# A state-space scan with a planner that writes the order: the carried column is copied later, GpSimd's product gets its own buffer, and the planner chooses its next step differently

## The chip, the cores and the metric

The kernel runs on one core of a Trainium2 chip. Five engines have a queue of instructions each and work through it in order: TensorE (PE in the profile; PEld are its weight loads), VectorE (DVE), ScalarE (ACT), GpSimd (POOL) and SyncE (SP), which here only issues DMAs. They wait for each other through semaphores. The metric is the time of one execution on the device, in microseconds, as the median of several runs.

## The reference

A layer with two parts, on `u` of 4 sequences x 2048 steps x 256, all in f32:

```python
x = u + ssm(layernorm(u))
out = x + moe(layernorm(x))

# ssm, per sequence; 512 inner channels, 16 states per channel
xi, z = split(v @ W_in.T + b_in)
dt_raw, B, C = split(xi @ W_x.T + b_x)            # 16, 16, 16 wide
delta = softplus(dt_raw @ W_dt.T + b_dt)
h[t] = exp(delta[t] * A) * h[t-1] + xi[t] * delta[t] * B[t]
y[t] = sum_n h[t] * C[t]
ssm = ((y + xi * D) * silu(z)) @ W_out.T + b_out

# moe: 4 experts that share Wi and Wo and differ by a rank-4 addition
w = top-2 of softmax(x @ Wg.T + bg)
moe = sum_e w_e * (relu(x @ Wi.T + low_e @ Bm_e) @ Wo.T)
```

## The kernel before, in words

**Tiles.** The 8192 steps are cut into 16 chunks of `TC = 512` steps, four chunks to a sequence. Inner channels lie on the partitions, in four blocks `d` of 128, and time lies along the free dimension. A *state* is one pair of channel block and state number, 128 channels x 512 steps; a chunk has 4 x 16 = 64 of them, the kernel 1024. The list `states` (line 775) sets their sequence: half a chunk has two channel blocks, and within it a group of four states is two state numbers of the one block and then of the other.

**One state.** ScalarE makes the decay `dA = exp(delta * A)` into one of three PSUM buffers (`decay`, 783). GpSimd makes `dBx = xdt * B` for two states at once (`enter`, 788). VectorE runs the recurrence with one scan instruction, written over `dA` (`scan`, 800). The scan begins from the last column of the same state in the chunk before, kept in the small tile `carry`; ScalarE copies that column there (`keep`, 822). The last chunk of a sequence (3, 7, 11, 15) copies nothing, and the first (0, 4, 8, 12) begins from zero. Then the result is multiplied by C (`read`, 814) and TensorE adds it, transposed, into the PSUM tile `y` (`sum_y`, 827). For one state in four (`shared`, 809: the first of each group) the scan writes to `hS` in SBUF, and GpSimd does the product with C, in place; for the other three VectorE does it, from PSUM into `hC` (three buffers).

**The rest of a chunk.** In front of the scans of a chunk stand its layer norm (statistics `st_a` on VectorE, `rstd` on GpSimd, `xn_a` on ScalarE), the input projection (`pin`), the projection `pdbc`, whose B and C rows go through DRAM and are loaded back spread over the partitions, and softplus over the whole chunk. The gate is made with silu. Behind the scans come the gating of `y` (`close_y`), the output projection `po` (`tail`), and the mixture of experts (`ffn`): a layer norm, the routing in small tiles (`plg`, `m`, `lowm`), and eight steps `k` of base and low-rank products (`pz`), relu (`h`), transposes (`phT`, `hT`) and a down product (`pf`). While the scans of chunk c run, the front of chunk c+1 and the mixture of experts of chunk c-1 are worked on by whatever engine has time. Exp and relu, softplus, and silu need different tables, so softplus and silu each stand between two `ACT_TABLE_LOAD`s.

**The order.** Nothing is reordered after recording: each engine executes in the order in which Python writes the instructions. The main loop (915 to 976) writes the scan's own instructions state by state. Everything else is a list of `Step`s (35), each with an engine, an assumed cost in us, the steps that it follows, and the PSUM banks it takes and gives. `Pacer` (45) keeps an assumed clock for each engine. `start` (74) says when a step could begin by these clocks; `ready` (127) says whether it falls in a window around VectorE's clock. `fill` (106), called twice per state, writes all steps that are ready: the first ready one of the first thread, again and again. `force` (139) writes what a certain step needs, for instance where the next chunk is due, and at the end of the program, first for the second-last store and then for the last.

**The place of the copy.** In the loop's turn `i` the copy for state `i - 1` is written first (921), then the scan of state `i`, then fillers, then the C product of state `i - 1`, then the decay of state `i + 2`, then fillers. The tile framework lets two engines read one PSUM bank only one behind the other, in the order of recording, so the C product of VectorE waits for the copy.

Of the kernel before, what the change touches and what calls it, by code (L numbers as in the profile page):

```python
# [8 lines left out]
F32 = mybir.dt.float32  # L9
AF = mybir.ActivationFunctionType  # L10
ALU = mybir.AluOpType
# [33 lines left out]
class Pacer:  # L45
# [60 lines left out]
    def fill(self):  # L106

        begin = self.now["dve"]
        again = True
        while again:  # L110
            again = False
            for thread in self.threads:
                for x in self.heads(thread):
                    if (x.engine != "dve" or self.fits(x, begin)) and self.ready(x):
                        self.write(x)
                        thread.remove(x)
                        again = True
                        break
                if again:
                    break  # L120
        self.threads = [t for t in self.threads if t]

    def fits(self, x, begin):
# [3 lines left out]
    def ready(self, x):  # L127
        t = self.start(x)
        if t is None:
            return False  # L130
        v = self.now["dve"]
        if self.quiet and x.engine == "act" and x.cost > self.MOST:
            return False
        if x.engine == "dve":
            t = max([y.end for y in x.after if y.engine != "dve"], default=0.0)
            return t + self.LATENCY + self.MARGIN <= v
        return t <= v + self.BEGIN[x.engine] and (t + x.cost <= v + self.END[x.engine] or t <= v - 0.5)

    def force(self, last):

# [20 lines left out]
def ssm_moe_layer_kernel(  # L161
# [154 lines left out]
    def layernorm_T(src, dst, name, then=None):  # L316

        q = {}

        def stats(j):  # L320
            if j == 0:
                q["mv"] = small.tile([P, NJ, 2], F32, tag=f"mv{name[0]}", name=f"mv_{name}")
            x = small.tile([P, 6], F32, tag="st", name=f"st_{name}_{j}")
            dve.bn_stats(x, src()[:, j, :])
            dve.bn_aggr(q["mv"][:, j, :], x)

        def rstd():

            ve = small.tile([P, NJ], F32, tag="ve", name=f"ve_{name}")
            q["rstd"] = small.tile([P, NJ], F32, tag="rstd", name=f"rstd_{name}")  # L330
            q["nmr"] = small.tile([P, NJ], F32, tag="nmr", name=f"nmr_{name}")
            pool.tensor_scalar_add(ve, q["mv"][:, :, 1], EPS)
            pool.tensor_tensor(q["rstd"], ve, mhalf, ALU.pow)
            pool.tensor_tensor(ve, q["mv"][:, :, 0], q["rstd"], ALU.mult)
            pool.tensor_scalar_mul(q["nmr"], ve, -1.0)

        def norm(j):
            q["xn", j] = work.tile([P, DM], F32, tag=f"xn{j}", name=f"xn_{name}_{j}", bufs=1)
            act.activation(
                q["xn", j], src()[:, j, :], AF.Identity,  # L340
                scale=q["rstd"][:, j : j + 1], bias=q["nmr"][:, j : j + 1],
            )

        def turn(k):
            q["pt", k] = mm_tile(f"pt_{name}_{k}")
            for j in range(NJ):
                pe.transpose(
                    q["pt", k][:, j * P : (j + 1) * P], q["xn", j][:, k * P : (k + 1) * P], ident
                )

        def out_(k):
            if k == 0:
                q["dst"] = dst()
            act.copy(q["dst"][:, k, :], q["pt", k])

        steps = [Step("dve", 0.54, lambda j=j: stats(j)) for j in range(NJ)]
        steps += [Step("pool", 1.75, rstd)]
        steps += [Step("act", 0.5, lambda j=j: norm(j), locks=j == 0) for j in range(NJ)]
        norms = steps[-1]
        turns = [  # L360
            Step("pe", 0.45, lambda k=k: turn(k), after=[norms], takes=1, unlocks=k == KM - 1)
            for k in range(KM)
        ]
        outs = [Step("act", 0.5, lambda k=k: out_(k), after=[turns[k]], gives=1) for k in range(KM)]
        if then:
            steps.append(then)
        return steps + turns + outs
# [16 lines left out]
    def front(c, norm, taken=()):  # L384
# [65 lines left out]
        ln = steps[-1]  # L450
        for x in steps[-2 * KM :]:
            x.after += taken
        steps.append(Step("pe", 1.75, p_dbc, after=[ln], takes=1))
        steps.append(Step("act", 0.57, a_dbc, gives=1))
        dbc = steps[-1]
        dts, ins = [], []
# [5 lines left out]
        for m in range(ND):  # L462
# [2 lines left out]

        steps += dts + [soft] + ins if c == 0 else ins + dts + [soft]
        xdts = [
            Step("pool", 1.27, lambda m=m: xdt(m), after=[soft, ins[2 * m + 1]]) for m in range(ND)
        ]
        steps += xdts  # L470
        gate = []
# [78 lines left out]
    def ffn(c):  # L550
# [163 lines left out]
        for x in steps[-2 * KM :]:  # L714
            x.after += held.get("x2T", [])
        steps += [
            Step("pe", 2.0, p_route, takes=1),
            Step("act", 0.21, low_),
            Step("dve", 0.34, logits),
            Step("act", 0.85, exp_),  # L720
            Step("dve", 1.9, softmax, gives=1),
            Step("pool", 1.0, top),
            Step("pool", 0.6, mask),
            Step("pe", 0.5, p_turn, takes=1),
            Step("act", 0.5, a_turn, gives=1),
# [7 lines left out]
        for k in range(NK + 1):  # L733

            low = Step(
                "pe", 1.06 if 0 < k < NK else 0.9, lambda k=k: p_low(k), after=bases[k : k + 1] + z1s[-1:]
            )
            steps.append(low)
            if k:
                hs.append(Step("act", 0.57, lambda k=k: a_relu(k - 1, 0), after=[low], gives=1))  # L740
                steps.append(hs[-1])
            if k < NK:
                z1s.append(Step("act", 0.57, lambda k=k: a_relu(k, 1), after=[low]))
                steps.append(z1s[-1])
            steps += bases[k + 1 : k + 2]
            if k:
                steps.append(Step("pe", 0.9, lambda k=k: p_hT(k - 1), after=[hs[-1]], takes=1))
                steps.append(Step("act", 0.5, lambda k=k: a_hT(k - 1), after=[steps[-1]], gives=1))
                copies.append(steps[-1])
            for j in range(NJ):  # L750
                if k == min(2 * j + 3, NK):
                    for h in range(2):
                        steps.append(
                            Step("pe", 1.75, lambda j=j, h=h: p_down(j, h), after=[copies[2 * j + 1]], takes=1 - h)
                        )
                    steps.append(Step("dve", 0.33, lambda j=j: add(j), after=[steps[-1]], gives=1))
# [43 lines left out]
    def scan(i):  # L800
        c, ib, d, n = states[i]
        init = 0.0 if c % CPB == 0 else carry[:, d, n : n + 1]
        out_ = dAs[i]
        if shared(i):
            out_ = hCs[i] = scanp.tile([P, TC], F32, tag="hS", name=f"hS_{i}", bufs=2)
        dve.tensor_tensor_scan(out_, dAs[i], dBxs.pop(i), init, ALU.mult, ALU.add)
        dAs[i] = out_

# [5 lines left out]
    def read(i):  # L814
        c, ib, d, n = states[i]
        if shared(i):
            pool.tensor_tensor(hCs[i], hCs[i], bcs[ib, 1][:, n % NN, :], ALU.mult)
            return
        hCs[i] = scanp.tile([P, TC], F32, tag="hC", name=f"hC_{i}", bufs=3)
        dve.tensor_tensor(hCs[i], dAs.pop(i), bcs[ib, 1][:, n % NN, :], ALU.mult)  # L820

    def keep(i):
        c, _, d, n = states[i]
        if (c + 1) % CPB:
            act.copy(carry[:, d, n : n + 1], dAs[i][:, TC - 1 : TC])

    def sum_y(i):

# [80 lines left out]
    for d in range(ND2):  # L909
        scale, turn = open_y(0, d)  # L910
        xd = pacer.run("act", 0.63, scale)
        pacer.run("pe", 0.5, turn, [xd])
    begin(0)
    xds, turn, summed = {}, None, []
    for i in range(M + 4):

        pacer.quiet = (i + 5) % (PER // NH) < 8
        if turn:
            pacer.run("pe", 0.5, *turn)
            turn = None  # L920
        if 1 <= i <= M:
            pacer.run("act", 0.15, lambda: keep(i - 1), [S[i - 1]])
        for e in (1, 4):

            if i + e < M + 3 and i + e >= 3:
# [5 lines left out]
        if 3 <= i < M + 3:  # L931
            c, _, d, n = states[i - 3]
            if n == N - 1:
                copy, *steps = close_y(c, d)
                steps[0].after = [pacer.run("act", 0.5, copy, [Y[i - 3]]), silus[c]]
                pacer.add(steps, first=True)
                gates.setdefault(c, []).append(steps[-1])
                turn = xds.pop((c + 1, d - ND2) if d >= ND2 else (c, d + ND2), None)
                if d == ND - 1:
                    begin(c + 1)  # L940
# [19 lines left out]
        if 1 <= i <= M:  # L960
            if shared(i - 1):
                C[i - 1] = pacer.run("pool", 1.23, lambda: read(i - 1), [S[i - 1]])
            else:
                C[i - 1] = pacer.run("dve", 0.6, lambda: read(i - 1), [S[i - 1], *summed[-3:-2]])
            if i + AHEAD_A < M:
                A[i + AHEAD_A] = pacer.run(
                    "act", 0.63, lambda: decay(i + AHEAD_A), [(S if shared(i - 1) else C)[i - 1]]
                )
        for late in (3, 2):
            if late <= i < M + late and (late == 3) == shared(i - late):  # L970
                Y[i - late] = pacer.run("pe", 0.5, lambda: sum_y(i - late), [C[i - late]])
                if late == 2:
                    summed.append(Y[i - late])
        if i < M:
            group(i)
        pacer.fill()
    pacer.force(before_last)
    pacer.force(last_out)


# [45 lines left out]
```

## Time and profile before

| | us |
|---|---|
| median of 3 runs | 2138.67 (2132.21 to 2139.30) |
| the profiled execution | 2132.56 |
| its span | 2130.8 |
| first to last scan | 31.8 to 2000.8 |
| behind the last scan | 130.0 |

| engine | busy us | share | instructions |
|---|---|---|---|
| TensorE | 1875.5 | 88% | 9504 |
| VectorE | 1848.2 | 87% | 2423 |
| GpSimd | 1708.3 | 80% | 1084 |
| ScalarE | 1427.2 | 67% | 2898 |

| costliest groups | count | mean us | busy us |
|---|---|---|---|
| GpSimd dBx | 512 | 2.365 | 1206.3 |
| VectorE scan into dA, from carry | 576 | 1.277 | 723.5 |
| ScalarE dA | 1024 | 0.690 | 704.3 |
| VectorE hC | 768 | 0.675 | 518.1 |
| GpSimd hS | 256 | 1.274 | 326.2 |
| ScalarE carry from dA | 576 | 0.156 | 89.7 |
| ScalarE table load | 64 | 1.283 | 82.1 |

How to read it: busy time is the time in which an engine executes. On VectorE and ScalarE an instruction that waits for nothing begins a little before the one ahead ends, so distances of starts are shorter than durations: 1.19 us for a scan of 1.28, 0.60 for a product of 0.67. A line of the waits says which engine stood idle before which instruction, and what released it at last. In the text chunks are counted from 0, states within a chunk from 0 to 63.

### The profile page before, as it was taken

What the parts mean: (1) busy time and instruction counts of PE and PEld (TensorE: products, weight loads), DVE (VectorE), ACT (ScalarE), POOL (GpSimd) and SP (SyncE); (2) the same over time, 40 slices, a digit from 0 to 9 for tenths busy, and PEclk for the clock granted to TensorE, in tenths of its full rate; (3) what the DMA queues carried; (4) which work ended last, traced back from release to release, by engine and by line L of the source; (5) the groups of instructions that cost most, each with busy time, mean ns of one, the idle gap of its engine ahead of it and who ended that gap; (6) DMA issues with size and microseconds to landing.
All of it is one profiled execution on the core that took longest, in us unless ns stands there. A gap on an engine that the chain in (4) does not pass through costs nothing. (4 is left out here: it accounts for less than half of the span.)

```text
span 2130.8 us, 28679 instructions
## 1 busy us (share of the span) xinstructions
PE 1875.5 (88%) x9504; PEld 1284.4 (60%) x9504; DVE 1848.2 (87%) x2423; ACT 1427.2 (67%) x2898; POOL 1708.3 (80%) x1084
## 2 busy tenths in 40 slices
PE   6768788798898898999999898988999899989878
PEld 3545556566566575656666565666657566666655
DVE  4899899999999999999999998989999899899510
ACT  5757667667767777766777776666777767766422
POOL 5898888889888887998898887879888888988400
PEclk9859799899899999999999998999999999999989
DMA  6444344444444453543544353444535444443100
GB/s 213 152 161 151 128 149 143 157 147 158 141 148 151 138 179 118 179 140 140 169 148 160 132 175 115 143 150 145 174 129 179 139 137 143 147 159 139 50 11 10
DMA packets 106133, 300.71 MB, mean 141 GB/s; under 512 B 12864, under 2 KB 39104, under 8 KB 105984
## 3 DMA queue, kind: packets, MB, share of 16 engines
q1 hardware_dynamic: 105984, 298.88, 41.3%
q8 instruction: 74, 1.21, 0.2%
q14 instruction: 75, 0.61, 0.1%
HBM read 289.41 MB, written 9.44 MB: 140 GB/s over the span
## 5 line engine op out<-in xcount | busy, mean ns | idle before, releaser
L30 POOL TENSOR_TENSOR dBx<-xdt,B 128x1024 f32<-128x1024 f32 x512 | 1206.3, 2365 | 92.3 <-DVE dA L30 38.0
L30 ACT ACTIVATE dA<-delta,a_sb 128x512 f32<-128x512 f32 x1024 | 704.3, 690 | 364.7 <-DVE hC L30 336.7
L30 DVE TENSOR_TENSOR_SCAN dA<-dA,carry,dBx 128x512 f32<-128x512 f32 x576 | 723.5, 1277 | 26.3 <-ACT carry L30 14.6
L30 DVE TENSOR_TENSOR hC<-dA,C 128x512 f32<-128x512 f32 x768 | 518.1, 675 | 84.8 <-ACT carry L30 81.8
L30 PE MATMUL y<-ident,hC 128*128 128x128 f32 x3072 | 486.6, 289 | 33.8 <-DVE hC L30 33.1
L30 PEld LDWEIGHTS y<-ident,hC 128*128 128x128 f32 x3072 | 384.2, 149 | 179.8 <-DVE hC L30 65.9
L30 POOL TENSOR_TENSOR hS<-hS,C 128x512 f32<-128x512 f32 x256 | 326.2, 1274 | 76.5 <-ACT carry L30 60.1
L30 PE MATMUL pz<-wi_sb,x2T 128*128 128x512 f32 x512 | 267.4, 648 | 17.4 <-ACT hT L30 11.3
L30 PE MATMUL pf<-wo_sb,hT 128*128 128x256 f32 x1024 | 244.7, 386 | 11.4 <-ACT hT L30 8.5
L30 PE MATMUL pin<-xnT,w_in_sb 128*128 128x512 f32 x512 | 246.0, 609 | 2.7 <-ACT lowT L30 1.1
L30 DVE TENSOR_TENSOR_SCAN hS<-dA,carry,dBx 128x512 f32<-128x512 f32 x192 | 243.9, 1270 | 3.2 <-ACT dA L30 3.1
L30 DVE TENSOR_TENSOR_SCAN dA<-dA,dBx 128x512 f32<-128x512 f32 x192 | 228.8, 1216 | 2.0 <-ACT carry L30 1.9
L30 ACT ACTIVATE h<-pz,topv 128x512 f32<-128x512 f32 x256 | 168.2, 686 | 89.2 <-PE pz L30 87.4
L30 PEld LDWEIGHTS pf<-wo_sb,hT 128*128 128x128 f32 x1024 | 188.5, 192 | 38.6 <-ACT hT L30 12.4
L30 PE MATMUL y<-ident,hS 128*128 128x128 f32 x1024 | 169.8, 292 | 39.5 <-POOL hS L30 39.5
L30 PEld LDWEIGHTS y<-ident,hS 128*128 128x128 f32 x1024 | 129.5, 149 | 119.7 <-POOL hS L30 54.8
L30 PEld LDWEIGHTS pz<-wi_sb,x2T 128*128 128x128 f32 x512 | 94.1, 205 | 129.1 <-issue 80.1
L30 PE MATMUL phT<-ident,h 128*128 128x128 f32 x1024 | 142.6, 283 | 29.5 <-ACT h L30 19.0
L30 PE MATMUL pz<-bm_sb,lowT 16*128 16x512 f32 x512 | 165.9, 653 | 0.0
L30 PEld LDWEIGHTS phT<-ident,h 128*128 128x128 f32 x1024 | 119.8, 145 | 57.3 <-ACT h L30 23.8
L30 PEld LDWEIGHTS pin<-xnT,w_in_sb 128*128 128x128 f32 x512 | 92.5, 198 | 83.2 <-issue 71.8
L30 PE MATMUL po<-w_out_sb,g 128*128 128x256 f32 x512 | 128.6, 401 | 5.7 <-DVE u L30 2.7
(94 smaller groups left out, 1750.9 us busy)
## 6 DMA issues: line engine op xcount, KB each, us to landing
B<-bc SPq DMA_DIRECT2D x256, 512.0 KB, 3.7
C<-bc SPq DMA_DIRECT2D x256, 512.0 KB, 3.8
ua<-in_u_dram SPq DMA_DIRECT2D x16, 512.0 KB, 5.6
u<-in_u_dram SPq DMA_DIRECT2D x16, 512.0 KB, 5.5
out_dram<-u SPq DMA_DIRECT2D x16, 512.0 KB, 3.4
w_in_sb<-in_w_inT_dram SPq DMA_DIRECT2D x2, 512.0 KB, 4.7
wi_sb<-in_wiT_dram SPq DMA_DIRECT2D x1, 1024.0 KB, 8.0
wo_sb<-in_woT_dram SPq DMA_DIRECT2D x1, 1024.0 KB, 11.2
```

The source lines that it names most:

```text
L30: return self._tc.keep_in_program_order(f(*args, **kwargs))
```

## The change

The copy of the column is written behind the product with C (behind GpSimd's product for the states that GpSimd multiplies), directly ahead of the next decay. GpSimd's product goes into a tile of its own, `hP`, with two buffers, in place of being written over `hS`. `hC` has four buffers, not three, and the product waits in the planner for the fourth-last sum, not the third-last. `fill` makes a list of all ready steps and writes the one whose engine would stand idle the least before it (0.25 us of idleness count as none; among equals the first thread wins). At the end `drain` takes over from the two calls of `force`: of all steps that can be written, the one that begins earliest. Silu of a chunk is forced before the chunk's first `y` is closed. Some assumed costs are changed. The program has the same compute instructions; the order is made anew throughout.

```diff
     def fill(self):
         begin = self.now["dve"]
-        again = True
-        while again:
-            again = False
-            for thread in self.threads:
-                for x in self.heads(thread):
-                    if (x.engine != "dve" or self.fits(x, begin)) and self.ready(x):
-                        self.write(x)
-                        thread.remove(x)
-                        again = True
-                        break
-                if again:
-                    break
+        while True:
+            due = [
+                (max(0.0, self.start(x) - self.now[x.engine] - 0.25), at, x)
+                for at, thread in enumerate(self.threads) for x in self.heads(thread)
+                if (x.engine != "dve" or self.fits(x, begin)) and self.ready(x)
+            ]
+            if not due:
+                break
+            _, at, x = min(due, key=lambda d: d[:2])
+            self.write(x)
+            self.threads[at].remove(x)
...
+    def drain(self):
+        while self.threads:
+            heads = [(x, t) for t in reversed(self.threads) for x in self.heads(t) if self.start(x) is not None]
+            x, thread = min(heads, key=lambda h: self.start(h[0]))
+            self.write(x)
+            thread.remove(x)
+            self.threads = [t for t in self.threads if t]
...
-        steps += [Step("pool", 1.75, rstd)]
+        steps += [Step("pool", 1.95, rstd)]
...
-            out_ = hCs[i] = scanp.tile([P, TC], F32, tag="hS", name=f"hS_{i}", bufs=2)
+            out_ = scanp.tile([P, TC], F32, tag="hS", name=f"hS_{i}", bufs=2)
...
     def read(i):
         c, ib, d, n = states[i]
         if shared(i):
-            pool.tensor_tensor(hCs[i], hCs[i], bcs[ib, 1][:, n % NN, :], ALU.mult)
+            hCs[i] = scanp.tile([P, TC], F32, tag="hP", name=f"hP_{i}", bufs=2)
+            pool.tensor_tensor(hCs[i], dAs[i], bcs[ib, 1][:, n % NN, :], ALU.mult)
             return
-        hCs[i] = scanp.tile([P, TC], F32, tag="hC", name=f"hC_{i}", bufs=3)
-        dve.tensor_tensor(hCs[i], dAs.pop(i), bcs[ib, 1][:, n % NN, :], ALU.mult)
+        hCs[i] = scanp.tile([P, TC], F32, tag="hC", name=f"hC_{i}", bufs=4)
+        dve.tensor_tensor(hCs[i], dAs[i], bcs[ib, 1][:, n % NN, :], ALU.mult)
...
-            act.copy(carry[:, d, n : n + 1], dAs[i][:, TC - 1 : TC])
+            act.copy(carry[:, d, n : n + 1], dAs.pop(i)[:, TC - 1 : TC])
...
-        if 1 <= i <= M:
-            pacer.run("act", 0.15, lambda: keep(i - 1), [S[i - 1]])
...
+                pacer.force(silus[c])
...
-                C[i - 1] = pacer.run("dve", 0.6, lambda: read(i - 1), [S[i - 1], *summed[-3:-2]])
+                C[i - 1] = pacer.run("dve", 0.6, lambda: read(i - 1), [S[i - 1], *summed[-4:-3]])
+            pacer.run("act", 0.1, lambda: keep(i - 1), [(S if shared(i - 1) else C)[i - 1]])
             if i + AHEAD_A < M:
                 A[i + AHEAD_A] = pacer.run(
...
-    pacer.force(before_last)
-    pacer.force(last_out)
+    pacer.drain()
```

The other assumed costs: `p_dbc` 1.75 to 1.86, `xdt` 1.27 to 1.23, `p_route` 2.0 to 1.75, `top` 1.0 to 1.1, the first and last `p_low` 0.9 to 1.05, `p_hT` 0.9 to 0.88, and 0.5 to 0.45 for `sum_y` and the opening transposes.

More of the change, by code (lines that the diff above doesn't have):

```diff
@@ L452, in front @@
             x.after += taken
-        steps.append(Step("pe", 1.75, p_dbc, after=[ln], takes=1))
+        steps.append(Step("pe", 1.86, p_dbc, after=[ln], takes=1))
         steps.append(Step("act", 0.57, a_dbc, gives=1))
@@ L467, in front @@
         xdts = [
-            Step("pool", 1.27, lambda m=m: xdt(m), after=[soft, ins[2 * m + 1]]) for m in range(ND)
+            Step("pool", 1.23, lambda m=m: xdt(m), after=[soft, ins[2 * m + 1]]) for m in range(ND)
         ]
@@ L716, in ffn @@
         steps += [
-            Step("pe", 2.0, p_route, takes=1),
+            Step("pe", 1.75, p_route, takes=1),
             Step("act", 0.21, low_),
@@ L721, in ffn @@
             Step("dve", 1.9, softmax, gives=1),
-            Step("pool", 1.0, top),
+            Step("pool", 1.1, top),
             Step("pool", 0.6, mask),
@@ L735, in ffn @@
             low = Step(
-                "pe", 1.06 if 0 < k < NK else 0.9, lambda k=k: p_low(k), after=bases[k : k + 1] + z1s[-1:]
+                "pe", 1.06 if 0 < k < NK else 1.05, lambda k=k: p_low(k), after=bases[k : k + 1] + z1s[-1:]
             )
@@ L746, in ffn @@
             if k:
-                steps.append(Step("pe", 0.9, lambda k=k: p_hT(k - 1), after=[hs[-1]], takes=1))
+                steps.append(Step("pe", 0.88, lambda k=k: p_hT(k - 1), after=[hs[-1]], takes=1))
                 steps.append(Step("act", 0.5, lambda k=k: a_hT(k - 1), after=[steps[-1]], gives=1))
@@ L911, in ssm_moe_layer_kernel @@
         xd = pacer.run("act", 0.63, scale)
-        pacer.run("pe", 0.5, turn, [xd])
+        pacer.run("pe", 0.45, turn, [xd])
     begin(0)
@@ L918, in ssm_moe_layer_kernel @@
         if turn:
-            pacer.run("pe", 0.5, *turn)
+            pacer.run("pe", 0.45, *turn)
             turn = None
-        if 1 <= i <= M:
-            pacer.run("act", 0.15, lambda: keep(i - 1), [S[i - 1]])
         for e in (1, 4):
@@ L970, in ssm_moe_layer_kernel @@
             if late <= i < M + late and (late == 3) == shared(i - late):
-                Y[i - late] = pacer.run("pe", 0.5, lambda: sum_y(i - late), [C[i - late]])
+                Y[i - late] = pacer.run("pe", 0.45, lambda: sum_y(i - late), [C[i - late]])
                 if late == 2:
```

## The prediction

> **What bounds the kernel now.** I read the busy table first, then the windows of one chunk each, then the waits of VectorE, then the timeline around the longest waits, then the chain that ends last.
>
> ```profile
> PE 1875.5 (88%) x9504; PEld 1284.4 (60%) x9504; DVE 1848.2 (87%) x2423; ACT 1427.2 (67%) x2898; POOL 1708.3 (80%) x1084
> ```
>
> No engine is full, so the bound must be read by stage. The scans run from 31.8 to 2000.8 us (1969.0 us, VectorE busy 1832.0); behind them stands a tail of 130.0 us with VectorE busy 11.8. The scan stage is VectorE's: idle 137.0 us. Windows of VectorE alone (stretch, length, busy, then clock and DMA) show where:
>
> ```profile
> 274.60:399.90 125.30, 116.26 (x152) 0.90 0.42 148
> 399.90:515.60 115.70, 113.55 (x140) 0.99 0.44 151
> 1385.70:1510.50 124.80, 116.17 (x153) 0.96 0.43 148
> ```
>
> These are chunks 2, 3 and 11. Chunks 3, 7, 11 and 15 end a sequence and copy no carried column. Their idle time is 2.2, 5.6, 8.6 and 5.4 us, 21.7 in all (mean 5.4). The twelve that copy have 115.3, mean 9.6. The waits of VectorE and one of GpSimd name the difference (total, times, longest):
>
> ```profile
> DVE hC L30 <- ACT carry L30: 81.8, 79, 6.1
> DVE dA L30 <- ACT carry L30: 16.4, 15, 2.9
> DVE dA L30 <- ACT dA L30: 10.0, 17, 1.4
> POOL hS L30 <- ACT carry L30: 60.1, 73, 4.3
> ```
>
> The C product waits for ScalarE's copy of one column, since both read the same PSUM tile and the copy is recorded first. ScalarE works in order, so whatever stands ahead of the copy holds VectorE. Silu in chunk 9, a carrying one (start, length):
>
> ```profile
> 1148.73 1.28 ACT L30 ACT_TABLE_LOAD   x1
> ...
> 1150.03 1.92 ACT L30 ACTIVATE g<-g 128x2048 f32<-128x2048 f32 x1
> ...
> 1151.95 1.28 ACT L30 ACT_TABLE_LOAD   x1
> 1153.24 0.69 ACT L30 ACTIVATE dA<-delta,a_sb 128x512 f32<-128x512 f32 x1
> 1153.87 0.15 ACT L30 COPY carry<-dA 128x1 f32<-128x1 f32 x1
> 1154.06 0.69 DVE L30 TENSOR_TENSOR hC<-dA,C 128x512 f32<-128x512 f32 x1 [2.29 <-ACT carry L30]
> ```
>
> ScalarE is held 4.5 us (1148.73 to 1153.24), and the product then waits for a decay and the copy behind it: 2.29 us lost. The same block at the same state of chunk 11, without copies, ends so:
>
> ```profile
> 1407.50 1.30 ACT L30 ACTIVATE dA<-delta,a_sb 128x512 f32<-128x512 f32 x2
> 1408.30 1.28 DVE L30 TENSOR_TENSOR_SCAN hS<-dA,carry,dBx 128x512 f32<-128x512 f32 x1 [1.18 <-ACT dA L30]
> ```
>
> Products went on; only the scan waited for its decay: 1.18 us. So the copy costs 1.1 us at such a block, and there are two blocks per chunk.
>
> **The change, part by part.** *The copy behind the product.* In the built program 576 C products wait for ScalarE before, none after. If carrying chunks idle like the others, 12 x (9.6 - 5.4) = 50 us go. Ends: 0 (the waits only change their name) and 98.2 (81.8 + 16.4, all of it). I take 50, the row of the chunks without copies being the nearest there is.
>
> What it adds: the copy now waits for the product, and the decay stands behind it. In a group of four states VectorE runs: scan 0, product of the last group's state 3, scan 1, scan 2, product 1, scan 3, product 2. The decay for scan 2 needed scan 0 alone; now the copy of the last group's state 3 is ahead of it on ScalarE. From that product's start: 0.67 product, 0.15 copy, 0.69 decay, three handovers of about 0.04 (scan 712 ended 1401.51, its decay began 1401.55): 1.63 us. Scan 2 is due 0.60 + 1.19 = 1.79 us after that start. The slack of this one decay falls from about 0.95 to 0.16; the others keep about 0.7, where the copy had some 0.2 twice a group. One decay per group, 16 groups, 12 chunks: 192 tight places. Ends: 0 if ScalarE is free each time, 192 x (0.69 - 0.16) = 102 us if an activation of 0.69 has always just begun. ScalarE is busy 1375.9 of 1969.0 us in this stage (70%), but most fillers are placed where the old order had slack; chunks without copies, with 0.16 to 0.95 us more slack, waited for decays 1.8 to 4.5 us per chunk. I take 0.05 us per place: +10.
>
> Also, 292 decays now wait for the copy directly ahead on their own engine: the next activation starts 0.15 + 0.03 instead of 0.04 us behind the copy (1144.44 to 1144.48), so 292 x 0.14 = 41 us more of ScalarE over twelve chunks, 3.4 each of 116, within its 30% idle: 0 on the path beyond the 10. Here the Trainium skill (ScalarE: Activation LUTs, What ACT_TABLE_LOAD costs) speaks against the change: back-to-back activations overlap by about 93 ns, which a wait for the instruction ahead gives up; by it the estimate is 292 x 0.09 = 27 us of ScalarE. The same section prices a table load at about 2.7 us; by it a block would last 7.3 us and the two blocks of every chunk would take 32 x 2.8 = 90 us more than the trace has. The trace has 1.28, and it decides.
>
> *GpSimd's own buffer hP.* Its wait of 60.1 us for the copy goes. GpSimd reaches VectorE through dBx and hS alone, and VectorE's waits for those are 3.8 + 1.4 + 0.2 = 5.4 us: gain 0 to 5.4. I take 0, as the 3.8 is the start of the first scan. *Fourth hC buffer:* the product's waits for TensorE are 1.0 us in all: 0 to 1.0, taken 0. *Silu forced before the y of its chunk closes:* in the new order silu stands at state 5 of its chunk from chunk 6 on, and the force falls at state 32, so it finds nothing to do: 0. *Step costs* move only the order.
>
> *The new fill rule.* The order is made anew on all engines, the loads of SP and GpSimd's small steps included. From chunk 7 on softplus stands at state 24 of every chunk and silu at state 5, where before they wandered from 12 to 17 and 28 to 39. At state 24 all four statistics pairs of the next chunk (4 x 0.5 us: 0.32 to 0.41 and 0.18) stand inside the block, so most of its loss is covered; silu at 5 has two gate products (0.67) and I expect 1.9 us lost. SP's loads of B and C stand some nine states ahead of their readers in both orders, and VectorE waited 1.4 us for them: 0. GpSimd's bias add stands further behind its load (its waits for that DMA were 25.9 us), which does not reach VectorE. The remaining idle time, 16 x 5.4 = 86, bounds the gain: at best chunk 3's 2.2 everywhere (-52); at worst chunk 10's 13.7 (its window 129.9, busy 116.2) everywhere (+133). Most of a chunk is as before, so I take -10.
>
> *The tail.* At the last scan the new program has two of FFN 14's eight steps less to do, and the first four matmuls of the output product come ahead of the last down product. A step costs (2106.98 - 2094.90) / 2 = 6.0 us:
>
> ```profile
> 2094.90 3.72 PE pf L30 x16
> ...
> 2106.98 3.72 PE pf L30 x16
> ```
>
> So -12, between 0 (TensorE ends the scans behind) and -12 - 6.3 (the output product `po`, 6.33 us, wholly beside other work). TensorE has room for it in the scans: 1744.7 busy of 1969.0.
>
> Sum: -50 + 10 + 0 - 10 - 12 = -62 against the profiled execution's 2132.6 us (span 2130.8, 1.8 around it): 2070.6. That execution lies at the low end of the runs (2132.21 to 2139.30, median 2138.67), so I say 2072 for a median.
>
> **The rivals.** *The decays become the wait (slower).* Place: the decay for scan 2 of each group. If ScalarE is late there by 0.37 us on average over the 192 places, 71 us come back and, with the forecast's 72 of gains, nothing is left; at 0.5 us, 96 come back: 2132.6 - 72 + 96 = 2157. For it: slack 0.16 against fillers of 0.6 to 0.7 us, 256 of them `h`, which waited 87.4 us for TensorE. Against: chunk 3 has the same fillers and 1.2 us of such waits.
>
> *GpSimd becomes the bound.* Busy 1696.4 in the stage, 106 us a chunk, against VectorE's 116; its own in-order waits (mv 29 without the last, m 37.5, the bias DMA 25.9) add 92: 1789, and its gaps between dBx (27.5 + 22.8) make 1839. That is only 80 below 1919 (1969 - 50 + 10 - 10), the stage I forecast; where its small steps bunch, VectorE waits for dBx. At 2 us a chunk it costs 32: 2104. Against: chunk 3 ran 115.7 us with the same GpSimd work.
>
> *The order sheds more.* All chunks near chunk 3: -50 + 10 - 52 - 12 = -104, or 2029. For it: chunk 3 did it under the old rule. Against: chunks 7, 11 and 15, also without copies, did not.
>
> *Nothing changes.* The product waits for something else at once (TensorE, C): that would be about 2132, but the second-latest release in those rows is not shown.
>
> **How the numbers follow.** Forecast (2045 to 2092): 0.52. More shed (2010 to 2045): 0.14. GpSimd (2092 to 2118): 0.17. Nothing, or a gain and a loss alike (2126 to 2139 counts as within 0.3% of 2132 to 2139): 0.04. Decays (above 2139): 0.13. A measurement of this kernel can tell about 0.3% (6 us). Faster 0.83, same 0.04, slower 0.13. For 8 in 10 I leave out the slower rivals and the lowest of the better one: 2030 to 2118.
>
> **What would show it.** Right: no wait of hC for carry; VectorE's idle time in carrying chunks near 6 us, now for dA; silu losing about 1.9 us and softplus under 0.6; hP waiting for no copy; TensorE's end 115 to 120 us behind the last scan; VectorE busy unchanged. Wrong: waits of dA for dA above 100 us; waits for dBx above 20 us; a tail still at 130.

## The result, and the profile after

The changed kernel takes 2130.14 us (median of 12 runs, 2126.37 to 2131.90), the kernel before, in 12 runs, 2137.99. The ratio is 0.9967, 95% interval 0.9955 to 0.9979: 0.3% faster, 8 us, where 2072 was forecast. The profiled execution took 2129.43 us (span 2127.7). Its busy table:

```profile
PE 1873.9 (88%) x9504; PEld 1284.0 (60%) x9504; DVE 1855.8 (87%) x2423; ACT 1441.7 (68%) x2898; POOL 1709.4 (80%) x1084
```

VectorE is busy 7.6 us longer with the same 2423 instructions. The windows of VectorE, the scan stage and what lies behind the last scan (stretch, length, busy, then clock and DMA):

```profile
31.60:2014.80 1983.20, 1839.58 (x2374) 0.93 0.45 148
2014.80:2127.70 112.90, 11.76 (x35) 0.91 0.03 10
```

The tail is 17.1 us shorter than before (130.0), and the scan stage 14.2 longer (1969.0). VectorE's idle time in the stage is 143.6 us, against 137.0. Its waits (total, times, longest):

```profile
DVE dA L30 <- ACT dA L30: 81.5, 129, 6.1
DVE hS L30 <- ACT carry L30: 21.0, 10, 6.5
DVE hS L30 <- ACT dA L30: 7.8, 8, 1.5
DVE dA L30 <- ACT carry L30: 4.3, 6, 1.4
DVE dA L30 <- POOL hP L30: 3.9, 6, 1.4
DVE hS L30 <- POOL dBx L30: 3.4, 1, 3.4
```

The row "hC waits for carry", 81.8 us before, is gone. "dA waits for dA", that is a scan waiting for its decay, has gone from 10.0 us in 17 waits to 81.5 in 129. A scan is the place to look then, and the scans' waits for their decays, sorted by the place of the state in its group of four (counted from 0.06 us on; the rows above leave out what is under 0.15), say which: place 0 has 11 waits (8.0 us), place 1 has 80 (41.1 us), place 2 has 22 (14.6), place 3 has 35 (26.7). Before, place 1 had 4 waits and 1.1 us. 64 of the 80 are alike, 0.18 us each; 13 are long (1.0 to 6.1 us, 29 us together). One of the alike, in chunk 9, in the timeline of the changed kernel (start, length; the scan into `hS` is place 0, the last line is place 1):

```profile
1225.54 1.27 DVE L30 TENSOR_TENSOR_SCAN hS<-dA,carry,dBx 128x512 f32<-128x512 f32 x1
1225.84 0.16 ACT L30 COPY carry<-dA 128x1 f32<-128x1 f32 x1
1226.73 0.66 DVE L30 TENSOR_TENSOR hC<-dA,C 128x512 f32<-128x512 f32 x1
1226.85 0.69 ACT L30 ACTIVATE dA<-delta,a_sb 128x512 f32<-128x512 f32 x1 [0.85 <-DVE hS L30]
...
1227.57 1.29 DVE L30 TENSOR_TENSOR_SCAN dA<-dA,carry,dBx 128x512 f32<-128x512 f32 x1 [0.18 <-ACT dA L30]
```

ScalarE is free at 1226.00, but its decay waits 0.85 us until the scan into `hS` has ended at 1226.81. The decay is for the very next scan, and only one product (0.66) lies between. So the decay comes 0.18 us too late.

Why does a decay wait for the scan just ahead of its own? Decays lie in three PSUM buffers. No line of the kernel names them; the framework chooses one for each decay when it builds the program. Its rule is not shown here, and the order of writing alone does not give it: the decay for place 1 is written one turn ahead of the scan of place 0. The built programs tell which decay got whose buffer. Of the last 240 groups:

| buffer of the decay at | before | after |
|---|---|---|
| place 1: of 3 states earlier | 240 | 160 |
| place 1: of the state just ahead | 0 | 80 |
| place 2: of 2 / of 4 states earlier | 240 / 0 | 160 / 80 |

A buffer of places 1 to 3 now stays in use until the copy, which is written later. In 80 groups place 1 then gets the buffer that the scan just ahead is still reading, and place 2 gets another one with it. I call these near groups. That this explains the time was a reading so far; the runs below test it.

### The profile page after: what moved, and what is told of

It reads as the page before. It is cut to its first block, busy times and chain, and to the rows that moved or that the text cites. A ratio compares the mean times of both kernels' runs of the same rounds, so it can differ in the third digit from the quotient of the medians.

```text
span 2127.7 us, 28591 instructions
## 1 busy us (share of the span) xinstructions
PE 1873.9 (88%) x9504; PEld 1284.0 (60%) x9504; DVE 1855.8 (87%) x2423; ACT 1441.7 (68%) x2898; POOL 1709.4 (80%) x1084
## 4 chain that ended last, share of the span: by engine, by line
PE 25%; DVE 20%; ACT 12%; issue 5%; POOL 1%; DVEq 0%; POOLq 0%; ACTq 0%
DVE dA L30 9%; PE pz L30 9%; PE y L30 5%; PE pf L30 5%; ACT dA L30 5%; DVE hC L30 4%; DVE hS L30 4%; PE phT L30 3%; ACT L30 2%; ACT h L30 1%; PE pin L30 1%; ACT delta L30 1%; ACT g L30 1%; DVE u L30 1%; DVE plg L30 1%
## 5 line engine op out<-in xcount | busy, mean ns | idle before, releaser
L30 POOL TENSOR_TENSOR hP<-hS,C 128x512 f32<-128x512 f32 x256 | 326.6, 1276 | 5.1 <-issue 4.1
L30 PE MATMUL pz<-wi_sb,x2T 128*128 128x512 f32 x512 | 271.7, 657 | 25.2 <-ACT hT L30 15.4
L30 PE MATMUL pf<-wo_sb,hT 128*128 128x256 f32 x1024 | 243.4, 383 | 11.6 <-ACT hT L30 9.4
L30 ACT COPY carry<-dA 128x1 f32<-128x1 f32 x576 | 90.1, 157 | 208.5 <-DVE hC L30 206.5
L30 PEld LDWEIGHTS y<-ident,hP 128*128 128x128 f32 x1024 | 128.3, 148 | 96.3 <-issue 56.7
L30 PE MATMUL y<-ident,hP 128*128 128x128 f32 x1024 | 167.1, 288 | 18.7 <-POOL hP L30 18.7
L30 PEld LDWEIGHTS pz<-wi_sb,x2T 128*128 128x128 f32 x512 | 95.2, 207 | 124.9 <-issue 76.2
## 6 DMA issues: line engine op xcount, KB each, us to landing
wo_sb<-in_woT_dram SPq DMA_DIRECT2D x1, 1024.0 KB, 10.4
```

Of the source, the lines that this page charges most:

```text
L30: return self._tc.keep_in_program_order(f(*args, **kwargs))
```

## The experiments

Each ratio is against runs of the kernel before on the same chip.

| kernel | median us | ratio, 95% interval | scan stage | tail |
|---|---|---|---|---|
| copy late, old order rules | 2130.30 | 0.9983 (0.9950 to 1.0017) | 1987.3 | 121.8 |
| after, copy early | 2119.45 | 0.9931 (0.9907 to 0.9955) | 1965.9 | 114.4 |
| after, end forced as before | 2131.13 | 0.9985 (0.9972 to 0.9998) | 1986.4 | 113.3 |
| after, buffers named | 2096.48 | 0.9832 (0.9809 to 0.9855) | 1950.4 | 112.4 |
| the same, one decay ahead of the copy | 2099.80 | 0.9836 (0.9808 to 0.9864) | 1955.3 | 112.6 |
| copy late, buffers named | 2068.81 | 0.9694 (0.9665 to 0.9722) | 1914.2 | 121.2 |
| before, no copies | 2075.48 | 0.9718 (0.9687 to 0.9750) | 1914.7 | 129.9 |
| after, no copies | 2070.68 | 0.9699 (0.9666 to 0.9733) | 1923.6 | 112.9 |
| copy late, named, new costs | 2081.79 | 0.9757 (0.9738 to 0.9776) | 1925.1 | 113.2 |
| copy late, named, new fill rule | 2063.29 | 0.9671 (0.9645 to 0.9697) | 1913.1 | 125.8 |
| copy late, named, all groups near | 2219.70 | 1.0394 (1.0376 to 1.0413) | 2060.4 | 126.3 |
| after, named, old costs | 2066.24 | 0.9683 (0.9662 to 0.9703) | 1908.1 | 124.9 |

Stage and tail are those of the profiled execution, which may lie some us off the median.

### The change taken apart

The late copy alone: the kernel before with only these edits (and `hP`, and a fourth `hC` buffer).

```diff
-        if 1 <= i <= M:
-            pacer.run("act", 0.15, lambda: keep(i - 1), [S[i - 1]])
...
+            pacer.run("act", 0.1, lambda: keep(i - 1), [(S if shared(i - 1) else C)[i - 1]])
```

> The kernel before with the later copy, the buffer hP and the fourth hC alone; planner's rule, costs and end as before. Theory A (the copy now holds the decay's PSUM buffer, so the waits move from the product to the scan): VectorE's waits of hC for carry go from 81.8 us to 0, its waits for decays come to 70 to 110 us, and the time stays within 0.5% of before, 2127 to 2147. Theory B (the copy's place gains the forecast 50 us, and the new order loses them): 2080 to 2095.

The reverse: the changed kernel with the copy back ahead of the product, the product in place in `hS`, and three `hC` buffers; fill rule, costs and end stay new.

> The changed kernel with the copy ahead of the scan as before, product in place in hS and three hC buffers; new rule, costs and end. Theory A: hC waits for carry as before, 80 to 110 us; the tail gains about 17 us, the order some us either way: 2110 to 2130. Theory B (the new order loses 50 us): 2155 to 2185.

The changed kernel with the old end:

```diff
-    pacer.drain()
+    pacer.force(before_last)
+    pacer.force(last_out)
```

> The changed kernel with the end of the program written as before (first what the second-last store needs, then what the last needs). If the end rule made the tail 17 us shorter (130 to 113 us behind the last scan): 2140 to 2150, with the same scan stage. If the tail is shorter because less of chunk 14's work is left when the scans end: 2130 to 2136.

Measured: the late copy alone is worth nothing that can be told (0.9983, its interval holds 1). Its waits of VectorE show the exchange of one wait for another:

```profile
DVE dA L30 <- ACT dA L30: 64.5, 110, 6.2
DVE hS L30 <- ACT carry L30: 26.1, 20, 2.3
DVE dA L30 <- ACT carry L30: 14.0, 11, 3.0
```

The built program has 81 near groups. The new order with the early copy has none; it gains 14 us (2119.45, against 2133.11), and its tail is 15.6 shorter. The changed kernel's ratio is 0.9967, not 0.9931: within the new order the late copy lost some 8 us, though the two intervals touch. The forced end leaves the tail at 113.3 against 112.9, so `drain` is not what shortens it. What the changed kernel won, it won behind the last scan.

### The buffers named

The decays take their buffers from a table that repeats the turn of the kernel before. Every engine's order stays that of the changed kernel, so only the buffers differ.

```diff
+    slots = [0, 1, 2, 0]
+    for i in range(4, len(states)):
+        slots.append(slots[i - (3, 3, 2, 4)[i % 4]])
...
-        dAs[i] = ps_a.tile([P, TC], F32, tag="dA", name=f"dA_{i}")
+        dAs[i] = ps_a.tile([P, TC], F32, tag=f"dA{slots[i]}", name=f"dA_{i}", bufs=1)
```

> The changed kernel, same order on every engine, but the decays' three PSUM buffers are given out by name, in the turn that the kernel before had, so that no decay takes the buffer of the state just ahead (80 of the last 240 groups do in the changed kernel). Theory C (these decays, which can begin only when the scan ahead has ended, hold the scans): VectorE's waits at the second state of a group fall from 41 us to about 20, time 2095 to 2115. If they are harmless: 2126 to 2134.

Measured: 2096.48, 34 us below the changed kernel (29 by the two ratios). Its scans wait less for their decays, though still long:

```profile
DVE dA L30 <- ACT dA L30: 66.4, 59, 6.1
```

At the second state of a group the waits fell from 41.1 us to 32.2, not to 20 as expected: the long ones stay. The two states at the same places, in this kernel's timeline:

```profile
1206.84 1.27 DVE L30 TENSOR_TENSOR_SCAN hS<-dA,carry,dBx 128x512 f32<-128x512 f32 x1
1207.14 0.16 ACT L30 COPY carry<-dA 128x1 f32<-128x1 f32 x1
1207.33 0.69 ACT L30 ACTIVATE dA<-delta,a_sb 128x512 f32<-128x512 f32 x1
1208.02 0.67 DVE L30 TENSOR_TENSOR hC<-dA,C 128x512 f32<-128x512 f32 x1
1208.61 1.29 DVE L30 TENSOR_TENSOR_SCAN dA<-dA,carry,dBx 128x512 f32<-128x512 f32 x1
```

The decay follows the copy at once, beside the scan into `hS`, and the next scan starts 1.77 us after it, not 2.03. The stage is 32.8 us shorter: VectorE has 7.3 us less busy time (1848.5 against 1855.8 in all), its scans wait 9 us less at place 1, 4 at place 2 and 2 at place 3. Since the order is the same, the two traces can be set side by side scan by scan: 21.8 of the 32.8 us lie in the near groups (13.4 from the first scan to the second, 8.0 from the second to the third), the rest outside them. TensorE's clock is a little higher (0.939, against 0.929), but ScalarE's waits for TensorE are not shorter (309.1 us, against 292.6). The slowest run with names, at 0.933, took 2100.90, and the fastest of the changed kernel, at 0.929, 2126.37: 25 us at nearly the same clock. The busy time is part of the price, since a scan that starts behind a wait loses its start beside the end of the instruction ahead (in the fence of after, the product starts at 1226.73 and the scan ahead of it ends at 1226.81: 0.08 us).

The tight decay that the prediction named, that for place 2, was tried on top of it: it is written ahead of the copy of the last group's place 3.

> The kernel with the buffers given out by name, and one more edit: the decay for the third state of a group, which takes the buffer that the group's first scan has freed, is written ahead of the copy of the last group's fourth state, not behind it. If that decay is the other tight place (0.16 us of slack; 13 waits with 10.4 us at the third state in the kernel with named buffers), those waits fall to about 4 us and the time to 2082 to 2092; the planner's order moves with it, some 5 us either way. If not, 2093 to 2100.

Measured: 2099.80, no gain (ratio 0.9836, against 0.9832). The waits for a decay at place 2 fell from 13 (10.4 us) to 7 (5.1), but waits for a copy took their place (27 at place 2, 11.6 us).

### The copies left out, and the late copy with named buffers

How much is there to win at all? Both kernels without any copy of a carried column; the scans of all chunks start from zeros, so the carried state, a part of the computation, is missing.

```diff
-        if (c + 1) % CPB:
+        if (c + 1) % CPB and c < 0:
```

> The kernel before without the copies of the carried column (the scans begin from a tile of zeros in their place, so the carry between chunks is left out); order of all else as the planner wrote it with them. This bounds what any place of the copy can win. By the chunks without copies (5.4 against 9.6 us idle): 2075 to 2095. If the decays limit anyway: 2110 to 2130.

> The changed kernel without the copies of the carried column (zeros in place of the carry between chunks). If the copy behind the product, with named buffers, is nearly free: within 10 us of the kernel with named buffers, 2083 to 2096. If the copy still costs in the decay's chain: 2060 to 2080.

And the late copy alone, with named buffers:

> The kernel before with the later copy, hP and the fourth hC buffer, old planner rule and end, and the decays' buffers given out by name as in the kernel before. If the later copy is worth what the forecast said once the buffers keep their turn (50 less 10 us): 2085 to 2100. If the buffers give back the same 33 us as in the changed kernel and the copy's place is worth no more: 2095 to 2105. If the rule is needed for it: 2115 to 2130.

Measured: without copies 2075.48 and 2070.68, with no near group in either. The late copy with named buffers takes 2068.81, as little as no copies at all. The same edit without names took 2130.3, so the late copy (with `hP`, the fourth `hC` buffer and the order that the planner makes of them) is worth 3.1%, and without names all of it was gone. 2068.81 is lower than any of the three expectations allowed (2085 or above). The changed kernel with names takes 26 us more than without copies: under its order and costs the copy is not free. The waits of VectorE in the kernel with names:

```profile
DVE dA L30 <- ACT dA L30: 37.9, 33, 6.1
DVE hS L30 <- ACT carry L30: 13.3, 12, 2.6
DVE dA L30 <- ACT carry L30: 9.9, 4, 3.0
```

Not all of this pair's difference need be the buffers alone: TensorE's granted clock was 0.911 in the profile of the late copy alone (2142.58 us, at the upper end of its runs) and 0.940 with names. The runs of the late copy alone at its highest clock, 0.924, took 2114.3 and 2114.8, still 42 us more than the slowest run with names (2072.0, at 0.936). The 0.012 of clock that is left between these is no small thing: within the late copy's own runs 0.013 went with 28 us. Set side by side scan by scan, 41 of the 73 us between the two stages lie in near groups.

### Every group near

If near buffers are the cause, more of them must cost more. The last kernel with another table, which gives place 1 the buffer of the state just ahead in every group:

```diff
-        slots.append(slots[i - (3, 3, 2, 4)[i % 4]])
+        slots.append(slots[i - (3, 1, 4, 4)[i % 4]])
```

> The late copy under the old planner with named buffers, but in every group the second state's decay takes the buffer of the first state, whose scan stands just ahead (240 of the last 240 groups; 81 do in the kernel with the late copy alone, 0 in the one with named buffers). If this neighbourhood is the whole cause: 81 groups cost 62 us (2130 against 2069), so three times as many cost 120 to 190 us: 2190 to 2260. If only the copies that hold a buffer late matter: 2069 to 2130.

Measured: 2219.70, 151 us more than with the table of before. Waits of VectorE, then of ScalarE:

```profile
DVE dA L30 <- ACT dA L30: 118.3, 267, 5.9
DVE dA L30 <- ACT carry L30: 34.6, 20, 4.0
```

```profile
ACT dA L30 <- DVE hS L30: 283.4, 243, 4.6
ACT carry L30 <- DVE hC L30: 165.9, 203, 3.2
```

ScalarE now waits for the scan into `hS` once per group. Place 1 has 177 waits for a decay (49.2 us; 10 and 18.8 with the other table), VectorE's busy time is 28.8 us longer (1871.7 against 1842.9), and the waits at place 2 rise from 18.3 to 79.7 us (for decays 8.1 to 44.8, for copies 10.2 to 34.9), probably since ScalarE works in order and what it does behind the late decay is late too; this was not tested apart. So the price of a near group is not its 0.18 us. It is 151 / 255 = 0.59 (the table makes every group near but the first), 34 / 80 = 0.42 in the changed kernel and 61.5 / 81 = 0.76 for the late copy alone, the last with the difference of clock named above. TensorE's clock is lower here too (0.910), but ScalarE's waits for TensorE did not grow (246.6 us against 252.0), while those for VectorE went from 312.9 to 492.2: the loss came through VectorE's scans. Why the clock is lower stays open.

### The fill rule and the costs

With names, the changed kernel (2096) is still slower than the late copy alone (2069), so its order loses something. The late copy with names, and only the changed step costs, or only the new fill rule:

> The late copy with named buffers (2069 us) and only the changed step costs added; old fill rule and end. If the costs lose the 27 us that the whole new planner loses on top of named buffers (2096 against 2069): 2088 to 2100. If the fill rule loses them: 2062 to 2076.

> The late copy with named buffers and only the new fill rule added; old costs and end. If the fill rule loses the 27 us: 2088 to 2100, with the waits of scans for decays near the 66 us of the full planner. If it is the costs: 2062 to 2076. If rule and costs each lose a part: 2076 to 2088.

And the changed kernel with names and only its step costs set back (here one of them):

```diff
-            Step("pe", 1.75, p_route, takes=1),
+            Step("pe", 2.0, p_route, takes=1),
```

> The changed kernel with named buffers (2096 us), with the step costs set back to those of the kernel before; fill rule, end rule and the forced silu stay. If the changed costs are what the new order loses: 2055 to 2072, like the rule alone (2063). If the end rule or the forced silu lose it: 2085 to 2100. The end rule was worth 1 us in the changed kernel, so the first is expected.

Measured: the costs alone lose 13 us (2081.79, between the two expectations). The rule alone takes 2063.29, the lowest median here, but the 5.5 us are not clear of noise: the ratios' intervals overlap (0.9645 to 0.9697 and 0.9665 to 0.9722), and one run took 2071.92. The changed kernel without the new costs takes 2066.24, 30 less than with them, at the same clock (0.938 and 0.939). The costs shorten the tail (124.9 to 112.4) and lengthen the stage by 42 us (1908.1 to 1950.4). The costs are only numbers in the planner; the instructions are the same, in another order. ScalarE's wait for one of the groups concerned, with the new costs and then with the old:

```profile
ACT hT L30 <- PE phT L30: 76.5, 79, 3.7
```

```profile
ACT hT L30 <- PE phT L30: 60.8, 62, 3.2
```

All of ScalarE's waits for TensorE are 309.1 us with the new costs and 237.8 with the old. That these waits are the cause is not shown: where the costs alone lose 13 us the sum did not grow (249.1, against 252.0), and the kernel before without copies has 313.4 at 2075. Which of the changed costs loses the time, and by which steps, was not taken apart.

## Why the prediction was wrong, point by point

**What bounds the kernel** was read rightly: the scan stage is VectorE's, and the product's wait for the copy was worth taking away. Without copies the kernel before gains 62 us, 54 of them in the scan stage; the forecast's row for it was 50.

**The copy behind the product, -50.** Here the prediction failed. The wait is gone as forecast, but carrying chunks idle as much as before: 117 us over twelve (9.8 each, forecast near 6, before 9.6). The step at fault is "If carrying chunks idle like the others": chunks without copies differ in one more thing, namely that no copy holds their buffers. In the built change the term is 0, its lower end ("the waits only change their name"). With the buffers named, the late copy gives -65 (3.06% of some 2135), of which 55 in the scan stage, where the forecast had -50 and +10 for the tight decay, -40 together. Two misses cover the 58 us between 2072 and 2130: the buffers (34) and the step costs (30, below). With both put right the changed kernel takes 2066.24. That this lies so near to 2072 is in part luck, as single terms missed by 5 to 15 us.

**The tight decay, +10.** At the place that it named the number came out: at place 2 the waits for decays went from 4.3 to 14.6 us, +10.3. But in the near groups place 2 has another buffer than the term assumed; with the buffers named it is 10.4, or +6.1. The sentence "the others keep about 0.7" was wrong. For place 1 it took the buffer's owner as unchanged. In 80 of 240 groups the decay had to wait for the scan just ahead, which by the prediction's own durations is 0.04 + 0.69 + 0.04 against a product of 0.60: a slack of -0.17, not 0.7, and in the timeline a wait of 0.18. The rival *the decays become the wait* had the right kind of wait and the wrong place; its cover, ScalarE being free, could not help, since ScalarE was free and not allowed to begin. The owner could have been read from the waits of the built program, where the decay at place 1 waits for the `hS` scan ahead of it.

**The wait for the copy directly ahead, 0.** It is there (a copy at 1207.14, its decay at 1207.33, 0.19 later; 0.18 forecast), and the late copy with named buffers, which has it too, was as fast as no copies, which speaks for 0 on the path under the old planner. The Trainium skill (ScalarE: Activation LUTs, What ACT_TABLE_LOAD costs) gives back-to-back activations an overlap of about 93 ns. The decay at 1205.37 in the kernel with named buffers, 0.69 long, is followed by an activation at 1206.00: an overlap of 0.06, a third less. The 2.7 us that the prediction takes from the same section are there the load, 1283 ns, with a drain of about 1380 ns; the traces agree on the load (1.28), and in the block of chunk 9 no such drain shows (load to 1150.01, silu from 1150.03).

**`hP`, `hC` and GpSimd, 0.** Right. `hP` waits for no copy, and the rival *GpSimd becomes the bound* falls: VectorE waits 3.4 us for `dBx` and 3.9 for `hP`, and GpSimd waits for VectorE instead:

```profile
POOL dBx L30 <- DVE dA L30: 157.3, 241, 3.3
```

It was 38.0 us in 57 waits before.

**The new fill rule and "step costs move only the order", -10.** With named buffers the rule alone gave -5.5, not clear of noise, so -10 is neither shown nor refuted. The costs were booked at nothing, without a reason given; they lost 30 us in the changed kernel with names and 13 under the old rule. Silu at state 5 costs 1.6 to 2.3 us per chunk (1.9 forecast); for softplus the forecast said under 0.6. The scan at state 24, the first behind it, waits 0 to 0.85 us in chunks 6 to 13 and 2.3 in chunk 14. With the scans up to state 28, which wait too, it is 1.4 to 3.3 us in chunks 6 to 14, so the statistics covered a part at most; whether the later waits are softplus's was not separated.

**The tail, -12.** It fell by 17.1, within the range given. The cause is as said: less of the mixture of experts is left at the last scan. The last down product of chunk 14 starts 30.0 us behind it, where it was 44.3: 14.3 of the 17.1. It goes with the changed costs: every kernel above that has them has a tail of 112.4 to 114.4, every other one 121.2 to 130.0. So the tail was bought with a longer stage.

**VectorE's busy time unchanged.** It rose by 7.6 us; 80 near groups at 0.08 us of lost overlap give 6.4.

**Nothing changes** (2132) is the time that came out, but not its mechanism: the product waits for nothing else (0.2 us in all); the scans do. None of the three signs of being wrong appeared: waits of `dA` for `dA` stayed under 100 (81.5), waits for `dBx` under 20 (3.4), the tail moved. What told was the sign of being right that stayed away, 6 us of idle time in carrying chunks.

## What to carry to other kernels

An instruction that is written later also holds its buffer longer, and where buffers are handed out from a pool, the next owner may be another one: before pricing a moved reader, find out which instruction frees the buffer of each tile on the path, in the built program of both kernels, and name the buffers if the turn matters. Take the row with the edit's own side effects as the nearest one, not one in which the moved instruction is absent. Assumed costs in a planner are part of a change: with the turn kept, the late copy and the new fill rule but the old costs, this kernel runs at 0.967 of before (0.9645 to 0.9697), better than both; the old rule with the same (0.9694) cannot be told from it.

## What was not expected

A wait of 0.18 us cost more than twice that in the end, 0.42 to 0.76 us per group. A part is lost overlap (from scan to scan 2.03, not 1.77 us); another is lateness at the scan after, 8.0 us of the 32.8 in the changed kernel. The rest lies outside the near groups and was not followed. And TensorE's granted clock went with the time even between runs of one kernel: the late copy alone took 2142 us at 0.911 and 2114 at 0.924, the changed kernel 2131.4 to 2131.9 at 0.925 and 2126.4 to 2129.5 at 0.929. Whether the clock follows from the work's spacing or sets it, these runs do not tell, so a part of each difference between kernels of unlike clock may be the clock's.
